# A two-layer kernel whose feed-forward transposes the next block's tokens between a block's two products

## The chip, the cores and the metric

The kernel runs on one core of a Trainium2 chip. The metric is device time in microseconds (us), the median of several runs. PE is the matmul engine (TensorE), PEld its weight loads, DVE is VectorE, ACT is ScalarE, POOL is GpSimd and SP is SyncE, which issues most of the DMA transfers.

## The reference

Two transformer-like layers on x of shape (4, 1024, 256), all in fp32, each half followed by a residual sum and a layer norm:

```python
x = _layernorm(x + ssd_forward(x, ...))          # state-space mixing, 2 heads of 128, state 64
h = gelu(x @ w1 + b1)                            # 256 -> 1024, exact gelu
x = _layernorm(x + (h @ w2 + b2))                # 1024 -> 256
x = _layernorm(x + linear_attention(x, ...))     # 16 heads, exponential features, causal in chunks
x = _layernorm(x + mixture_of_experts(x, ...))   # 2 shared experts and the best 2 of 8, 512 hidden
```

The change is in the second line pair: the feed-forward of the first layer.

## The kernel before, in words

The 4096 tokens are eight blocks of 512 tokens (`xs[i]`, token tiles of 128 on the partitions). Each block goes through five groups of steps. `ssd_block` (lines 286 to 438) is the state-space part. `ffn_block` (lines 441 to 487) is the feed-forward. `attn_front` and `attn_back` (lines 499 to 759) are the attention, in half-blocks `hb` of 256 tokens, and `attn_tail` (line 761) routes the tokens. After them come the shared experts (`shared_jobs`, line 943) and, in a stage of its own, 69 tiles of routed tokens (`slot_tiles`, line 1023), which begins 1046 us into the profiled execution.

In everything up to that stage, PE's order is written out by a planner. A `Task` (line 249) has a cost, a rank, the tasks that it comes after, each with a wait in us, and the number of PSUM banks that it takes from one of two pools: pool 0 has six banks (SSD and attention), pool 1 has two (the feed-forward, later the shared experts). `trace_tasks` (line 255) keeps a clock of its own. It always takes the task that can start first by that clock, with ties decided by the lower rank, and a bank that a task used counts as free `hold` us after the task's end. The costs and waits are numbers in the source. PE executes the resulting order strictly; the orders of DVE, ACT and POOL follow from it. A task may hand back work for a later time (`rest`): the exponentials of the attention's features, `powers` on line 591, are issued 2.5 or 1.5 us of the planner's clock behind their task.

A feed-forward block is nine tasks:

- `turn_x` (line 444): eight PE transposes bring the block's 512 tokens into `ps_txT`, two banks of pool 1 with four transposes each. ACT copies each bank into the tile `xT`, of which there is one.
- four times `hidden` (line 449): two of the eight first products each (`ps_h`, lines 453 and 456). ACT applies gelu and writes a slice of `hT`, of which there is also one.
- four times `outputs` (line 458): the eight second products of one token tile (`ps_f`, line 465). Two token tiles share a bank, and DVE adds the bank to x (line 473). The last one runs the layer norm.

`before` is the previous block in the order 0, 2, 1, 3, 4, 5, 6, 7. A block's `turn_x` comes after the last `outputs` of the block before it, and its rank is 10 + i, behind all of the attention's ranks (5 to 7). The rank of a `hidden` is 10 + i + 0.1 n, that of an `outputs` 10.5 + i + 0.1 j.

Names used later: `ps_p` (line 577) are the attention's feature products, four banks at a time, first for the keys and then for the queries, cleared by ACT (line 589) and DVE (line 587). ACT then takes exponentials of them (lines 594 and 596). `ps_sc` (line 631) are the scores, masked by DVE, in one case of four by an ACT copy and POOL (lines 640 and 641). `ps_o` (line 670) uses them. `ps_to`, `ps_oT` and `ps_w` (lines 715, 728, 735) normalise, transpose and project the result.

Of the kernel before, what the change touches and what calls it, by code (L numbers as in the profile page):

```python
# [76 lines left out]
def two_layers(ctx: ExitStack, tc: tile.TileContext, x, xT, vecs, cols, wx, w1, w2, wqkv, wout, om, rw, moe, out):  # L77
# [19 lines left out]
    def bank(name, n):  # L97

        return psum[n].tile([P, 512], F32, tag="bank", name=name)
# [100 lines left out]
    def transposed(t, i, tiles, n, engines):  # L200


        width = len(tiles) * P
        engines = list(engines)
        for c0 in range(0, KC, 512 // width):
            chunks = range(c0, min(KC, c0 + 512 // width))
            ps = bank(f"ps_t{t.name}_{c0}", n)
            at = 0
            for c in chunks:
                for j in tiles:  # L210
                    nc.tensor.transpose(ps[:, at : at + P], xs[i][:, j, c * P : (c + 1) * P], ident)
                    at += P
            engines.pop(0)(t[:, c0 : chunks[-1] + 1, :].rearrange("p c t -> p (c t)"), ps[:, :at])
        return t

    def layernorm(i, by_act=False):

        st = sm.tile([P, NT, 6], F32, tag="ln_st", name=f"ln_st{i}")
        mv = sm.tile([P, NT, 2], F32, tag="ln_mv", name=f"ln_mv{i}")
        v = sm.tile([P, NT], F32, tag="ln_v", name=f"ln_v{i}")  # L220
        for j in range(NT):
            nc.vector.bn_stats(st[:, j, :], xs[i][:, j, :])
            nc.vector.bn_aggr(mv[:, j, :], st[:, j, :])
        nc.vector.tensor_scalar_add(v, mv[:, :, 1], LN_EPS)
        r = rsqrt(v, [P, NT], "ln")
        if by_act:
            nc.vector.scalar_tensor_tensor(v, mv[:, :, 0], -1.0, r, ALU.mult, ALU.mult)
            for j in range(NT):
                nc.scalar.activation(
                    xs[i][:, j, :], xs[i][:, j, :], AF.Identity, bias=v[:, j : j + 1], scale=r[:, j : j + 1]  # L230
                )
            return
        for j in range(NT):
            nc.vector.tensor_scalar(
                xs[i][:, j, :], xs[i][:, j, :], mv[:, j, 0:1], r[:, j : j + 1], ALU.subtract, ALU.mult
            )
# [44 lines left out]


    states = [None] * NB
    ssd_end, ffn_end, proj_end, turn_end, tail_end = {}, {}, {}, {}, {}

    def ssd_block(i, wk):

# [153 lines left out]
    def ffn_block(i, before, wk):  # L441
        v = SimpleNamespace(ps=None)

        def turn_x():
            v.xT = wk.tile([P, KC, TB], F32, tag="xT", name=f"xT{i}")
            transposed(v.xT, i, range(NT), 1, (nc.scalar.copy, nc.scalar.copy))
            v.hT = wk.tile([P, HID0 // P, TB], F32, tag="hT", name=f"hT{i}")

        def hidden(ms):
            for m in ms:  # L450
                ps = bank(f"ps_h{i}_{m}", 1)
                for k in range(KC):
                    nc.tensor.matmul(  # L453
                        ps, w1_sb[:, k, m * P : (m + 1) * P], v.xT[:, k, :], start=(k == 0), stop=(k == KC - 1)
                    )
                nc.scalar.activation(v.hT[:, m, :], ps, AF.Gelu, bias=col[:, m : m + 1])  # L456

        def outputs(j):
            if j == 0:
                b2 = vec0[:, _VEC["b2"]].unsqueeze(1).to_broadcast([P, NT, D])  # L460
                nc.gpsimd.tensor_add(xs[i], xs[i], b2)
            if j % 2 == 0:
                v.ps = bank(f"ps_f{i}_{j}", 1).rearrange("p (s d) -> p s d", s=2)
            for m in range(HID0 // P):
                nc.tensor.matmul(  # L465
                    v.ps[:, j % 2, :],
                    v.hT[:, m, j * P : (j + 1) * P],
                    w2_sb[:, m, :],
                    start=(m == 0),
                    stop=(m == HID0 // P - 1),  # L470
                )
            if j % 2 == 1:
                nc.vector.tensor_add(xs[i][:, j - 1 : j + 1, :], v.ps, xs[i][:, j - 1 : j + 1, :])
            if j == NT - 1:
                layernorm(i)

        r = 10.0 + i
        last = Task(turn_x, 0.9, r, [(ssd_end[i], 10.0), (before, 0.0)], 1, 2)
        wait = 4.0
        for n in range(4):  # L480
            last = Task(lambda n=n: hidden(range(2 * n, 2 * n + 2)), 3.5, r + 0.1 * n, [(last, wait)], 1, 2, 2.2)
            wait = 0.0
        wait = 3.0
        for j in range(NT):
            last = Task(lambda j=j: outputs(j), 3.5, r + 0.5 + 0.1 * j, [(last, wait)], 1, (j + 1) % 2, 2.2)
            wait = 0.0
        ffn_end[i] = last
# [683 lines left out]
    with tc.manual_schedule(engines={mybir.EngineType.PE}):  # L1171
# [8 lines left out]
        before = None  # L1180
        ffn_order = [0, 2, 1, 3, 4, 5, 6, 7]
        for i in ffn_order:
            ffn_block(i, before, wkf)
            before = ffn_end[i]
        constants = Task(attn_constants, 0.0, 4.0, [(ssd_end[0], 0.0)])
        spaces = SimpleNamespace()

# [32 lines left out]
        last = Task(open_second, 0.0, 0.0, [(ffn_end[ffn_order[-1]], 0.0)])  # L1220
        wait, jobs = 20.0, []
        for i, _, cost, n, banks, _ in shared_jobs(early + amid, None, None, None, banks_of, 2):
            after = [(last, wait), (turn_end[i], 3.0)]
# [3 lines left out]
            last, wait = jobs[-1], 0.0  # L1227
# [31 lines left out]
        wait = 6.0  # L1259
        for _ in range(2 * NTOK // P // 8 + 1):  # L1260
            sending = Task(lambda: spaces.steps.pop(0)(), 0.0, 0.0, [(sending, wait)])
            wait = 3.6
# [14 lines left out]
    with tc.manual_schedule(  # L1277
# [7 lines left out]
        parts, n = [], -1  # L1285
# [94 lines left out]
```

## Time and profile before

| | |
|---|---|
| median of 3 runs | 1547.89 us (1545.16 to 1551.54) |
| the profiled execution, its own time | 1545.36 us |
| its span, first to last instruction | 1543.5 us |
| mean granted PE clock | 0.991 |
| PE busy | 1485.6 us, 96% of the span |
| DVE, ACT, POOL busy | 752.8, 601.4, 418.5 us |
| first routed tile (`ps_ge`) starts | 1045.9 us |
| `xT` copies on ACT | 16, median 586 ns |
| gelu's table loads on ACT (line 456) | 28, 1283 ns each |

The profiled execution is one run; its time is 1.9 us more than its span, and 2.5 us less than the median of the three timed runs. A row of the window table gives the busy time of each engine in a stretch of the span, and the granted clock of PE there. In the timeline a row stands for a merged group of instructions, and the brackets give the idle time ahead of it and what ended it. A busy PE can still be slow: at half the granted clock an instruction simply takes twice as long.

### The profile page before, as it was taken

The page shows a single profiled execution, that of the slowest core. Times are in us where ns is not written, and L with a number is a line of the kernel's source. Part 1 is how long each engine was busy: PE and PEld are TensorE (multiplying, and loading weights), DVE is VectorE, ACT ScalarE, POOL GpSimd, SP SyncE. Part 2 cuts the span into 40 slices and gives each one's busy share as a digit, 9 for nine tenths or more (in the row PEclk, how much of TensorE's full clock was granted, in tenths as well). Part 3 has the DMA queues.
Part 4 walks back from the last instruction along what each step waited for, and adds up shares of the span by engine and source line. Part 5 has one row for each costly group of instructions (what it writes and reads, how often), then busy time and mean ns, then how long its engine had stood idle before and what let it go on. Part 6 is the DMA issues. An engine that isn't in the chain of part 4 may idle for free. (4 is left out here: it accounts for less than half of the span.)

```text
span 1543.5 us, 25320 instructions
## 1 busy us (share of the span) xinstructions
PE 1485.6 (96%) x9704; PEld 964.3 (62%) x9704; DVE 752.8 (49%) x2322; ACT 601.4 (39%) x1054; POOL 418.5 (27%) x456
## 2 busy tenths in 40 slices
PE   9999989999999989999999999999999999999997
PEld 5666657666766665755766665655666666666554
DVE  6977735774757474765636364112222222222264
ACT  3465374536464546355447311112222222222132
POOL 5723302322222121222110022103444444443200
PEclk9999999999999999999999999999999999999999
DMA  9000000000000000200101061222323233232331
GB/s 330 4 1 1 1 1 1 28 2 1 29 1 22 8 20 10 97 29 1 49 8 56 15 270 44 102 76 42 48 46 46 45 48 45 46 46 37 93 102 55
DMA packets 50197, 73.54 MB, mean 48 GB/s; under 512 B 8448, under 2 KB 42752, under 8 KB 48544
## 3 DMA queue, kind: packets, MB, share of 16 engines
q1 hardware_dynamic: 36128, 52.06, 9.5%
q0 software_dynamic: 13248, 18.17, 7.7%
q8 instruction: 80, 1.31, 0.4%
q10 hardware_dynamic: 704, 1.70, 0.3%
q14 instruction: 37, 0.30, 0.1%
HBM read 45.93 MB, written 25.99 MB: 47 GB/s over the span
## 5 line engine op out<-in xcount | busy, mean ns | idle before, releaser
L1033 PE MATMUL ps_ge<-w,xeT 128*128 x552 | 248.5, 593 | 1.0 <-issue 1.0
L961 PE MATMUL ps_g<-xTs,w 128*128 128x512 f32 x512 | 228.2, 599 | 2.2 <-ACTq L1087 0.8
L961 PEld LDWEIGHTS ps_g<-xTs,w 128*128 128x128 f32 x512 | 96.8, 193 | 117.2 <-issue 107.9
L1033 PEld LDWEIGHTS ps_ge<-w,xeT 128*128 128x128 f32 x552 | 99.5, 190 | 100.6 <-issue 100.6
L1064 POOL DMA_INDIRECT acc<-ye,back x69 | 109.3, 1585 | 110.5 <-DVE xew L1020 75.9
L1043 DVE TENSOR_TENSOR ge<-se,ps_ge 128x512 f32<-128x512 f32 x69 | 47.5, 688 | 178.8 <-PE ps_ge L1033 175.9
L1055 PE MATMUL ps_ye<-w2e,geT 128*128 x552 | 130.7, 380 | 0.9 <-DVE geT L1050 0.9
L1008 POOL DMA_INDIRECT xe<-xt,sent x69 | 68.0, 986 | 228.7 <-PE ps_xe L1016 166.3
L453 PE MATMUL ps_h<-xT,w_sb 128*128 128x512 f32 x256 | 117.9, 604 | 4.8 <-ACT hT L456 4.7
L979 PE MATMUL ps_e<-w,gT 128*128 128x256 f32 x512 | 114.6, 380 | 2.1 <-DVE x L988 2.1
L465 PE MATMUL ps_f<-w_sb,hT 128*128 128x256 f32 x512 | 115.9, 380 | 0.0
L641 POOL TENSOR_TENSOR sc<-sc,mask_le 128x512 f32<-128x512 f32 x32 | 40.7, 1272 | 270.3 <-ACT sc L640 270.3
L979 PEld LDWEIGHTS ps_e<-w,gT 128*128 128x128 f32 x512 | 96.1, 190 | 18.9 <-DVE x L988 3.7
L1055 PEld LDWEIGHTS ps_ye<-w2e,geT 128*128 128x128 f32 x552 | 99.6, 190 | 12.2 <-ACT ye L1063 1.1
L465 PEld LDWEIGHTS ps_f<-w_sb,hT 128*128 128x128 f32 x512 | 95.6, 190 | 15.4 <-issue 3.4
L970 DVE TENSOR_TENSOR gT<-sl,ps_g 128x512 f32<-128x512 f32 x64 | 43.9, 686 | 122.4 <-PE ps_g L961 95.2
L969 ACT ACTIVATE sl<-ps_g 128x512 f32<-128x512 f32 x64 | 38.1, 597 | 158.2 <-PE ps_g L961 144.9
L1041 ACT ACTIVATE se<-ps_ge 128x512 f32<-128x512 f32 x69 | 41.2, 597 | 121.6 <-PE ps_ge L1033 121.6
L453 PEld LDWEIGHTS ps_h<-xT,w_sb 128*128 128x128 f32 x256 | 47.7, 193 | 57.4 <-issue 47.0
L643 DVE TENSOR_TENSOR sc<-ps_sc,mask_le 128x512 f32<-128x512 f32 x96 | 63.1, 684 | 37.3 <-PE ps_sc L631 31.6
L631 PE MATMUL ps_sc<-qf,kf 64*128 64x128 f32 x1024 | 68.3, 284 | 0.9 <-DVE kf L587 0.5
L1063 ACT ACTIVATE ye<-ps_ye,xew 128x256 f32<-128x256 f32 x69 | 32.6, 473 | 92.9 <-PE ps_ye L1055 92.9
(268 smaller groups left out, 2445.0 us busy)
## 6 DMA issues: line engine op xcount, KB each, us to landing
w<-in_moe SPq DMA_DIRECT2D x8, 1024.0 KB, 8.6
x<-in_x SPq DMA_DIRECT2D x8, 512.0 KB, 10.8
xt<-x SPq DMA_DIRECT2D x8, 512.0 KB, 3.6
td<-xTr SPq DMA_DIRECT2D x16, 256.0 KB, 2.5
w2e<-in_moe SPq DMA_DIRECT2D x8, 512.0 KB, 7.6
x<-acc SPq DMA_DIRECT2D x8, 512.0 KB, 8.8
xt<-in_xT SPq DMA_DIRECT2D x7, 512.0 KB, 11.1
out<-x SPq DMA_DIRECT2D x7, 512.0 KB, 2.9
```

Source lines behind the costliest of these rows:

```text
L453: nc.tensor.matmul(ps, w1_sb[:, k, m * P : (m + 1) * P], v.xT[:, k, :], start=(k == 0), stop=(k == KC - 1))
L465: nc.tensor.matmul(v.ps[:, j % 2, :], v.hT[:, m, j * P : (j + 1) * P], w2_sb[:, m, :], start=(m == 0), stop=(m == HID0 // P - 1),)
L631: nc.tensor.matmul(ps[s][:, r * P : (r + 1) * P], kf[rows, r, q, tok], qf[rows, r, q, tok], start=True, stop=True)
L643: nc.vector.tensor_mul(t_s, ps_s, mask)
L961: nc.tensor.matmul(ps[s], w[e][:, 2 * s + k, m * P : (m + 1) * P], xT[i][:, k, :], start=(k == 0), stop=(k == KC - 1),)
L970: nc.vector.tensor_mul(gT[i, e][:, m, :], sl, ps[1])
L979: nc.tensor.matmul(ps, gT[i, e][:, m, j * P : (j + 1) * P], w2e[:, m, :], start=(e == 0 and m == 0), stop=(e == NSH - 1 and m == HID // P ...
L1008: nc.gpsimd.indirect_dma_start(out=xe, out_offset=None, in_=xt, in_offset=bass.IndirectOffsetOnAxis(ap=sent[:, s : s + 1], axis=0),)
L1033: nc.tensor.matmul(pg[a], xeT[s][:, k, :], w13[:, bass.ds(e * (4 * HID) + (2 * a + k) * HID, HID)], start=(k == 0), stop=(k == KC - 1),)
L1043: nc.vector.tensor_mul(ge[s], se, pg[1])
L1055: nc.tensor.matmul(ps[:, :D], geT[s][:, m, :], w2[:, bass.ds(of[s] * (2 * HID) + m * D, D)], start=(m == 0), stop=(m == HID // P - 1),)
L1064: nc.gpsimd.indirect_dma_start(out=acc, out_offset=bass.IndirectOffsetOnAxis(ap=back[:, s : s + 1], axis=0), in_=ye, in_offset=None, compu ...
```

## The change

A block's `turn_x` no longer comes after the last second product of the block before, but after that block's last first product, and its rank falls by 0.8, so that at equal time it goes ahead of that block's second products. The first `hidden` of a block now waits explicitly for the last `outputs` of the block before. Nothing is computed differently, and the exponentials that are issued late are as they were.

```diff
-        last = Task(turn_x, 0.9, r, [(ssd_end[i], 10.0), (before, 0.0)], 1, 2)
+        last = Task(turn_x, 0.9, r - 0.8, [(ssd_end[i], 10.0), (hid_end.get(before), 0.0)], 1, 2)
         wait = 4.0
         for n in range(4):
-            last = Task(lambda n=n: hidden(range(2 * n, 2 * n + 2)), 3.5, r + 0.1 * n, [(last, wait)], 1, 2, 2.2)
+            after = [(last, wait)] + [(ffn_end.get(before), 0.0)] * (n == 0)
+            last = Task(lambda n=n: hidden(range(2 * n, 2 * n + 2)), 3.5, r + 0.1 * n, after, 1, 2, 2.2)
             wait = 0.0
+        hid_end[i] = last
...
-            before = ffn_end[i]
+            before = i
```

Since the planner's clock decides what comes next, the order of everything behind the second block's `turn_x`, attention and shared experts included, is drawn up anew.

More of the change, by code (lines that the diff above doesn't have):

```diff
@@ L283, in two_layers @@
     states = [None] * NB
-    ssd_end, ffn_end, proj_end, turn_end, tail_end = {}, {}, {}, {}, {}
+    ssd_end, hid_end, ffn_end, proj_end, turn_end, tail_end = {}, {}, {}, {}, {}, {}
     def ssd_block(i, wk):
```

## The prediction

> **What bounds the kernel now.** I read the page first:
>
> ```profile
> span 1543.5 us, 25320 instructions
> PE 1485.6 (96%) x9704; PEld 964.3 (62%) x9704; DVE 752.8 (49%) x2322; ACT 601.4 (39%) x1054; POOL 418.5 (27%) x456
> ...
> PE   9999989999999989999999999999999999999997
> ```
>
> PE is busy for 96% of the span, and in no stretch below 70%. The change moves PE instructions and removes none, so it can only touch the 58 us in which PE is idle, and what its clock loses. Next the window table, over the stretches in which the PE timeline shows its longer gaps:
>
> ```profile
> core 0: us, PE busy (x) PEld busy (x) DVE busy (x) ACT busy (x) POOL busy (x), PEclk, DMA share, GB/s
> 184.00:220.00 36.00, 29.66 (x214) 16.51 (x215) 16.26 (x36) 31.08 (x43) 3.26 (x2) 0.91 0.00 1
> 325.00:355.00 30.00, 25.41 (x164) 15.43 (x164) 18.58 (x41) 17.43 (x28) 8.32 (x8) 0.94 0.00 1
> 430.00:450.00 20.00, 18.19 (x195) 10.72 (x196) 8.10 (x15) 17.83 (x27) 5.91 (x6) 1.00 0.01 1
> 595.00:615.00 20.00, 17.42 (x105) 10.98 (x105) 10.08 (x24) 17.20 (x25) 4.56 (x4) 1.00 0.02 1
> 680.00:697.00 17.00, 14.49 (x75) 8.15 (x74) 9.27 (x28) 15.36 (x23) 1.27 (x1) 0.92 0.01 0
> 805.00:825.00 20.00, 17.10 (x90) 9.20 (x83) 12.03 (x31) 19.13 (x28) 0.00 (x0) 0.91 0.15 52
> ```
>
> Where PE idles, ACT is mostly 86 to 96% busy, against 39% over the span. These are the places where feature exponentials, gelus (or the shared experts' activations) and the table loads between them fall together. The granted clock is 0.91 to 0.94 in four of them. Third, one such place in the timelines of PE and ACT:
>
> ```profile
> 193.01 1.09 PE L562 MATMUL ps_qkT<-ident,qk 128*128 128x128 f32 x8
> 196.04 5.32 PE L453 MATMUL ps_h<-xT,w_sb 128*128 128x512 f32 x8 [1.94 <-ACT hT L456]
> ```
>
> ```profile
> 193.28 0.71 ACT L596 ACTIVATE kf<-kf,ecap 128x512 f32<-128x512 f32 x1
> 194.00 1.28 ACT L456 ACT_TABLE_LOAD   x1
> 195.30 1.26 ACT L456 ACTIVATE hT<-ps_h,col 128x512 f32<-128x512 f32 x2
> ```
>
> ```profile
> 196.00:200.00 4.00, 3.96 (x6) 1.78 (x7) 0.54 (x1) 3.97 (x6) 0.00 (x0) 0.58 0.01 4
> ```
>
> PE stands for 1.94 us until a gelu frees a bank; the gelu stands behind exponentials and a table load. Then PE runs at 0.58 of its clock for 4 us, which loses another 0.42 x 4 = 1.7 us. Such a dip takes 1.7 us off 50 us, so a 50 us window with one has clock 0.97; five such windows have 0.97 and one (650 to 700) has 0.93: seven dips, 12 us. Last, PE's waits by releaser:
>
> ```profile
> PE ps_h L453 <- ACT hT L456: 4.7, 3, 2.0
> PE ps_o L670 <- POOL sc L641: 4.1, 2, 2.6
> PE ps_p L577 <- DVE kf L587: 3.2, 2, 2.5
> PE ps_oT L728 <- DVE o L721: 3.1, 2, 2.7
> PE ps_txT L211 <- DVE x L473: 2.0, 2, 1.7
> ```
>
> What this change aims at is the last row: a turn that waits for the second products' bank, 2.0 us in all. The planner keeps 4.0 us between turn and first product, but at block 2 the trace has the last transposes ending at 136.9 us and the first products from 137.2 us: nothing is lost there.
>
> **The change part by part.** Nothing is added to PE: per turn the same 8 transposes and 2 ACT copies of 586 ns, no DMA, nothing on POOL. In the instruction order of the changed kernel the seven later turns stand 23 to 43 us of PE work ahead of their block's first products, where it was 0.5 to 6 us. The last second product of block 7 comes some 20 us of PE work earlier, and with it SP's loads of the shared experts' weights; their first products have other work in front of them in either order. In the last part the order is looser: the dispatch's products (line 932) stand 14 us of PE work later, with 40 us left to the first routed tile. In the trace they ended at 993 us and the 512 KB loads of `w2e` that they release were issued by 997 us and landed in 12.3 us at most. So 40 us cover this; without cover it would be up to 16 us. ACT gets 90 table loads for 88, 2.6 us, beside PE.
>
> The rest is counted by cover: the PE work, in start-to-start times of the trace of before (0.86 us for a 512-wide fp32 product, 3.45 for eight second products, 0.49 for four transposes), that stands between producer and consumer, in both orders. The waits that should go:
>
> - The turn's wait for the bank of the second products: 0.35 us (block 1) and 1.67 us (block 6). 2.0 us.
> - At 213.9 us PE waits 2.56 us for POOL's masked scores; cover 4.0 us becomes 7.6. With the dip behind it 2.6 + 1.7 = 4.3 us.
> - At 252.5 us `ps_oT` waits 2.70 us with 1.2 us of cover, made up of block 3's turn; the new order has 3.7 there. 2.7 us.
> - At 335.7 us the query features wait 2.51 us for banks of the key features: cover 1.95 becomes 4.4. With the dip 4.2 us.
> - At 560.6 us and 645.3 us `ps_w` waits 1.76 and 1.20 us behind covers of 0 and 2.6; both become 5.05. 3.0 us.
>
> Together 16.2 us. The waits that should come:
>
> - A block's second products now stand behind the turn, in a bank that the turn's first copy must clear. For turns 3, 6 and 7 there are 3 to 6 us of cover; for turns 2, 1, 4 and 5 only the second four transposes, 0.49 us. With ACT free the copy takes 0.59 us and a start of some 0.1, so at least 0.2 to 0.3 us is lost. But ACT is in order: ahead of the copy at turn 4 stand two gelus and four copies (wait 0.8 us), at turn 5 a clearing of features, a table load of 1.28, an exponential of 0.72 and another clearing, 3.8 us against 1.0 of PE work (wait 2.7 us). I take 0.3 + 0.4 + 0.8 + 2.7 = 4.2 us; bounds 1.2 (ACT free) and 8 (two waits more like turn 5's). Behind PE's waiting instruction all of attention's products stand.
> - Does a wait of 2.7 us bring a dip? The trace says yes: of the waits of 1.9 us and more listed here all but the one at 252.5 us were followed by one. The Trainium skill, "TensorE: Matmul & The Clock Gate", section "What's actually happening", says that half rate comes after at least one idle window of about 3.4 us; by that rule neither this wait nor any listed here would cost more than itself. With the rule the sum below would be 12.8 us gone against 10.5 come, a gain of 2.3 us instead of 0.6; the measured dip decides. 1.7 us.
> - In half-block 9, `ps_oT` follows `ps_to` with 0.22 us of cover. In the trace 1.94 us passed without a wait and 1.2 waited 2.7; so 1.7 to 3.7 us, taken at 2.0 since DVE is less loaded there, plus a dip, 3.7 us.
> - Scores to `ps_o`: covers 1.9, 2.6 and 2.6 at three tiles, where 2.9 passed in the trace: 1.7 us.
> - Block 1's hidden products still fall among the features of half-blocks 0 and 1, now with 3.3 us between products in one bank instead of 4.3: 1.0 us more.
> - Hot ACT stretches: six before and six after, elsewhere. Counted by the measured durations of what ACT has to do between two of PE's instructions, the worst goes from 27.6 to 29.2 us of ACT work in 25 us of PE work: 1.6 us and a dip, 3.3 us.
>
> Together 4.2 + 1.7 + 3.7 + 1.7 + 1.0 + 3.3 = 15.6 us. Of the table loads a page speaks too: "ScalarE: Activation LUTs", section "What ACT_TABLE_LOAD costs", has 1283 ns and a drain of 1380 for each. The trace agrees on the load, but the exponential before it ended at 193.99 and the gelu began at 195.30: no drain is to be seen. By the page turn 5 would wait 4.1 us instead of 2.7; I keep the trace.
>
> Sum: 1545.4 (the profiled execution) - 16.2 + 15.6 = 1544.8 us. That execution was 2.5 us under the median of the runs, so 1547.3, say 1547 us.
>
> **The rivals.** *Faster: the new places do not stall.* Only the copies at the turns cost (5.9 us), and the other 9.7 us stay covered, because the real PE runs slower than the planner's clock and so gives more cover than asked. Then -16.2 + 5.9 = -10.3, 1537.6 us. For it speaks that covers of 1.94 us passed three times at `ps_oT`; against it the count of hot ACT stretches, six and six.
>
> *Slower: the stalls belong to ACT, not to the order.* ACT's stretches of features, gelus and table loads are as many as before, so each of the four attention waits that I let go (14.2 us) returns at another consumer in the same stretch, and only the turn's 2.0 us are gained. Then -2.0 + 15.6 = +13.6, 1561.5 us. It decides from 58% of the 14.2 us on: (7.7 + 0.6) / 14.2. For it speaks the window table, in which the gaps follow ACT's load whatever the consumer; against it the waits at 252.5 and 560.6 us, which were plain lack of cover.
>
> *The change does not do what it says*: the turn was no wait worth speaking of, the first products still wait for the second ones of the block before, and the reshuffle cancels. That is part of the middle case.
>
> **How the numbers follow.** About 0.5%, 7.7 us, is what a measurement of this kernel can tell from no change. The middle case (-0.6 us, its own range 1540 to 1555) has 0.41, the slower one 0.34, since an order that is drawn up anew also holds waits that I did not find, while I listed those of before in full; the faster one 0.25. The range of 1534 to 1560 reaches most of the way to both ends: all the new waits hidden but the copies' lower bound (-16.2 + 1.2, 1532.9) and all attention waits returned (1561.5).
>
> **What would show it.** In the profile of the changed kernel: the row of `ps_txT` waiting for DVE's x is gone; `ps_f` has waits for ACT's xT copy, 4 us in total, the longest at block 4's first second product; `ps_oT` has one wait of about 2 us some 630 us in; PE busy less dips is as before, with five to nine dips. The first `ps_ge` starts between 1038 and 1053 us and the rest takes 498 us as now. It would be wrong if `ps_ge` starts before 1038 (the faster case), or if `ps_h`, `ps_p` and `ps_k` wait longer in total than before while ACT's stretches stay above 90% (the slower case).

## The result, and the profile after

The changed kernel takes 1574.18 us (median of 5 runs, 1573.29 to 1577.03), against 1545.16 us for the kernel before on the same chip: 1.0184 times as long, 95% interval 1.0168 to 1.0200. The forecast was 1547 us, with a range of 1534 to 1560. It was wrong: the change costs some 28 us. The page of the changed kernel has

```profile
span 1571.4 us, 25316 instructions
PE 1498.6 (95%) x9704; PEld 971.2 (62%) x9704; DVE 750.5 (48%) x2322; ACT 606.0 (39%) x1056; POOL 419.1 (27%) x456
...
PE   9999989998899998989989999999999999999998
...
PEclk9999989999999999999999999999999999999999
```

The span is 27.9 us longer. PE has the same 9704 matmuls, but stands idle for 72.8 us instead of 57.9 (+14.9) and is busy for 1498.6 us instead of 1485.6 (+13.0). Equal work that takes longer is a matter of the clock: a first product's matmul takes 429 ns from start to start, and 853 in a stretch at half rate. In the trace's clock records before the routed tiles, the kernel before has 7 such stretches, each of 3.4 us, 24 us in all; the changed one has 12, six of them of 6.8 us, 61 us in all. PE is busy for 54 us of them instead of 23. Half of the difference, 15 us, is an estimate of what they cost, enough for the 13.0.

The first `ps_ge` starts at 1073.9 us instead of 1045.9. What follows takes 497.5 us, as it did. All of the loss thus lies in the part whose order the planner writes. PE's waits there, by what released them (total us, times, longest us):

```profile
PE ps_f L465 <- ACT xT L213: 8.1, 4, 5.7
PE ps_k L656 <- DVE qkT L567: 6.3, 4, 2.3
PE ps_g L964 <- ACT sl L972: 3.9, 3, 1.8
PE ps_oT L731 <- DVE o L724: 3.8, 4, 2.3
PE ps_w L738 <- ACT oT L733: 3.8, 2, 2.1
PE ps_e L982 <- DVE gT L973: 3.3, 1, 3.3
PE ps_k L656 <- DVE kf L590: 3.3, 1, 3.3
```

The row of `ps_txT` waiting for x is gone, as intended. In its place stands the second product's wait for the turn's copy, 8.1 us. Four more rows have grown or are new. In the kernel before, three of them were

```profile
PE ps_k L653 <- DVE qkT L564: 2.7, 1, 2.7
PE ps_w L735 <- ACT oT L730: 1.8, 1, 1.8
PE ps_g L961 <- ACT sl L969: 0.2, 1, 0.2
```

and `ps_e` had only its 2.1 us for x. Of waits over 1.5 us there are 15 with 36.3 us, where there were 13 with 27.1 (the one of 1.5 us at the kernel's very start, in both, is left out here and below).

The window table, over stretches of 50 us and of 20:

```profile
core 0: us, PE busy (x) PEld busy (x) DVE busy (x) ACT busy (x) POOL busy (x), PEclk, DMA share, GB/s
350.00:400.00 50.00, 43.81 (x417) 32.72 (x417) 28.33 (x71) 23.11 (x37) 9.67 (x9) 0.93 0.01 1
650.00:700.00 50.00, 42.55 (x418) 26.66 (x418) 25.43 (x65) 30.95 (x47) 6.50 (x7) 0.90 0.07 23
495.00:515.00 20.00, 16.26 (x123) 9.83 (x121) 10.36 (x24) 19.87 (x29) 1.77 (x2) 0.91 0.08 27
578.00:598.00 20.00, 14.05 (x73) 7.98 (x72) 14.87 (x39) 18.72 (x27) 3.34 (x3) 0.89 0.07 27
667.00:687.00 20.00, 14.99 (x72) 8.36 (x71) 12.99 (x36) 18.88 (x26) 3.52 (x3) 0.83 0.07 26
```

Before, the worst window of 50 us had a clock of 0.93; now three have 0.90 and three 0.93, of which the first two rows are examples. ACT is 46 and 62% busy in these two, but 94 to 99% in the three rows of 20 us, as it was in such places before. This parts the long waits in two. Those that end within some 20 us in which ACT is over 90% busy were 8 with 17.8 us before, and are 8 with 17.1 us now, at other places of the order. All other waits over 1.5 us rose from 9.3 to 19.1 us, and two of them, 5.7 and 3.3 us long, are 9.0 us, nearly the whole of that rise. These two come next.

**Turn 5, the longest wait.** The timelines of PE, ACT and DVE:

```profile
349.99 1.15 PE L580 MATMUL ps_p<-qkT,om_sb 32*128 32x256 f32 x16
351.07 1.09 PE L211 MATMUL ps_txT<-ident,x 128*128 128x128 f32 x8
357.85 5.42 PE L465 MATMUL ps_f<-w_sb,hT 128*128 128x256 f32 x16 [5.69 <-ACT xT L213]
```

```profile
351.20 0.69 ACT L592 ACTIVATE kf<-ps_p,fcap 128x512 f32<-128x512 f32 x1 [4.67 <-PE ps_p L580]
351.90 1.28 ACT L597 ACT_TABLE_LOAD   x1
356.02 0.72 ACT L597 ACTIVATE kf<-kf,fbias 128x512 f32<-128x512 f32 x1 [2.84 <-DVE kf L590]
356.65 0.67 ACT L592 ACTIVATE kf<-ps_p,fcap 128x512 f32<-128x512 f32 x1
357.22 1.06 ACT L213 COPY xT<-ps_txT 128x512 f32<-128x512 f32 x2
```

```profile
352.52 1.77 DVE L527 TENSOR_SCALAR ss<-ss 128x64 f32<-128x64 f32 x1
355.19 0.80 DVE L590 TENSOR_SCALAR kf<-ps_p,fcap,ffloor 128x512 f32<-128x512 f32 x1
```

Read it from the end. PE's second product waits for the copy; ACT had the transposes from 352 us on, but in front of the copy stands an exponential, which waits 2.84 us for the features that DVE clears; and DVE clears them only at 355.19, behind the norm of the queries and keys. Three queues, each in order, hand on the delay: PE stands behind ACT and ACT behind DVE, and neither PE's nor ACT's own work makes it. Then PE runs slowly:

```profile
355.00:362.00 7.00, 4.15 (x11) 3.42 (x12) 4.33 (x11) 4.10 (x7) 2.07 (x2) 0.55 0.01 2
```

**The shared experts, at the end.** One wait lies in a part that the forecast had called covered:

```profile
968.72 3.19 PE L982 MATMUL ps_e<-w,gT 128*128 128x256 f32 x14
975.23 4.98 PE L982 MATMUL ps_e<-w,gT 128*128 128x256 f32 x14 [3.33 <-DVE gT L973]
```

```profile
970.63 1.21 DVE L908 TENSOR_TENSOR in_lane<-lane_no,lane 128x1024 f16<-128x1024 f32 x1
971.77 1.67 DVE L900 TENSOR_TENSOR in_tile<-tile_no,its 128x568 f16<-128x568 f32 x1
973.37 1.21 DVE L908 TENSOR_TENSOR in_lane<-lane_no,lane 128x1024 f16<-128x1024 f32 x1
974.50 0.67 DVE L973 TENSOR_TENSOR gT<-sl,ps_g 128x512 f32<-128x512 f32 x1
```

PE's gate products end at 968.9, and the last product `gT` that DVE makes of them starts 5.6 us later, behind the comparisons that build the dispatch's masks. The rows of those comparisons, before and after (duration min/median/max in ns, first and last start in us):

```profile
L905 DVE TENSOR_TENSOR in_lane<-lane_no,lane x8: 1205/1212/1549, 916.4 to 935.5; 128x1024 f16<-128x1024 f32 x8
```

```profile
L908 DVE TENSOR_TENSOR in_lane<-lane_no,lane x8: 1204/1212/1772, 954.0 to 973.4; 128x1024 f16<-128x1024 f32 x8
```

Before, they were done at 937 us, while the gate products of a block still had 9 us to go:

```profile
937.35 8.85 PE L961 MATMUL ps_g<-xTs,w 128*128 128x512 f32 x20 [0.45 <-DVE gT L970]
```

Now they reach 5.7 us past the end of such a block. From 950 to 972 us DVE has no free moment:

```profile
950.00:972.00 22.00, 21.91 (x58) 10.67 (x57) 22.00 (x35) 3.58 (x6) 13.13 (x7) 1.00 0.68 275
```

### The profile page after: what moved, and what is told of

It reads as the page before. It is cut to its first block, busy times and chain, and to the rows that moved or that the text cites. A ratio compares the mean times of both kernels' runs of the same rounds, so it can differ in the third digit from the quotient of the medians.

```text
span 1571.4 us, 25316 instructions
## 1 busy us (share of the span) xinstructions
PE 1498.6 (95%) x9704; PEld 971.2 (62%) x9704; DVE 750.5 (48%) x2322; ACT 606.0 (39%) x1056; POOL 419.1 (27%) x456
## 5 line engine op out<-in xcount | busy, mean ns | idle before, releaser
L465 PE MATMUL ps_f<-w_sb,hT 128*128 128x256 f32 x512 | 119.7, 389 | 8.1 <-ACT xT L213 8.1
L634 PEld LDWEIGHTS ps_sc<-qf,kf 64*128 64x128 f32 x1024 | 61.9, 194 | 11.2 <-issue 5.6
## 6 DMA issues: line engine op xcount, KB each, us to landing
xt<-in_xT SPq DMA_DIRECT2D x7, 512.0 KB, 11.1
```

The costliest lines, as they stand in the source:

```text
L465: nc.tensor.matmul(v.ps[:, j % 2, :], v.hT[:, m, j * P : (j + 1) * P], w2_sb[:, m, :], start=(m == 0), stop=(m == HID0 // P - 1),)
L634: nc.tensor.matmul(ps[s][:, r * P : (r + 1) * P], kf[rows, r, q, tok], qf[rows, r, q, tok], start=True, stop=True)
```

## The experiments

All times are medians; the ratio is to the kernel before, measured beside it, with its 95% interval. "Over before" in the text is the ratio less one, times 1545.2 us, so that kernels measured at different times can be set side by side; two such values are told apart from some 4 us on.

| kernel | us | ratio |
|---|---|---|
| after | 1574.18 | 1.0184 (1.0168, 1.0200) |
| e2 new order, turns at their old place | 1576.97 | 1.0192 (1.0164, 1.0220) |
| e5 old order, turns moved | 1557.23 | 1.0075 (1.0058, 1.0092) |
| e9 as e5, turns in pool 0 | 1552.11 | 1.0046 (1.0030, 1.0063) |
| e18 after, turns in pool 0 | 1564.01 | 1.0110 (1.0085, 1.0134) |
| e3 after, copies on VectorE | 1577.47 | 1.0204 (1.0177, 1.0231) |
| e4 / e6 after / before, exponentials at once | 1565.58 / 1556.66 | 1.0128 (1.0100, 1.0155) / 1.0076 (1.0059, 1.0092) |
| e15 / e16 after / before, exponentials 0.5 us late | 1568.44 / 1551.19 | 1.0136 (1.0113, 1.0159) / 1.0040 (1.0019, 1.0061) |
| e10 / e11 after / before, Relu | 1546.88 / 1534.66 | 1.0001 (0.9990, 1.0012) / 0.9928 (0.9910, 0.9946) |
| e13 / e14 as e5 / as e2, Relu | 1533.62 / 1549.92 | 0.9912 (0.9891, 0.9934) / 1.0018 (1.0009, 1.0027) |
| e7, e8 before, one planner number changed | 1550.97, 1553.41 | 1.0036 (1.0022, 1.0050), 1.0043 (1.0026, 1.0060) |
| e12 after, floor on GpSimd | 1576.04 | 1.0195 (1.0174, 1.0215) |
| e17 after, no lane masks | 1571.74 | 1.0166 (1.0141, 1.0191) |

### e1, e5 and e2: the move and the order, each alone

The change does two things: it puts seven turns elsewhere, and it makes the planner draw up everything behind them anew. To part them, a hand-written step moves or puts back the turns after the planner is done. The loop itself is the same in e1 and e5:

```diff
+        for x, y in zip(ORDER, ORDER[1:]):
+            order.remove(turns[y])
+            at, cover = order.index(firsts[x]) + 1, 0.0
+            while cover < 2.2 and order[at] is not seconds[x]:
+                cover += order[at].cost
+                at += 1
+            order.insert(at, turns[y])
+            turns[y].start, turns[y].end = order[at - 1].start, order[at - 1].end   # e5 only
```

> PE's order of before, in which only the seven later turns are taken out and put behind the last first product of the block before (two tasks or so behind it, at the latest ahead of that block's second products). Theory A, the redrawn order of all the rest costs the time: 1541 to 1553 us, since the turn alone brings its copies' waits (about 4 us) and saves 2. Theory B, the turn between the two products costs it, through the bank that its copy must clear: 1565 to 1577 us, with ps_f waiting 8 us or more for ACT's xT.

e1 came to 1569.48 us, 1.0145. But in e1 a moved turn kept its planned start, and the late exponentials go by that clock, so that some were issued at wrong points and the kernel no longer computes the same. It decides nothing here. e5 gives the moved turn the start of its new neighbour.

> As the first kernel of the turn moved alone, but with the moved turn given the planned time of its new place, so that the late exponentials keep their places. Theory A (the redrawn order costs the time, the turn's place does not): 1543 to 1556 us, with ps_f waiting 4 to 8 us for ACT's copies. Theory B (the turn between the products is a cost of its own besides the order): 1560 to 1572 us.

e5: 1557.23 us, 11.6 us over before, between the two theories' ranges. The second products wait for ACT's copy in it as well:

```profile
PE ps_f L488 <- ACT xT L214: 10.0, 4, 4.5
```

e2 takes the new order and puts the turns back behind the last second product of the block before.

```diff
+        for x, y in zip(ORDER, ORDER[1:]):
+            order.remove(turns[y])
+            order.insert(order.index(ffn_end[x]) + 1, turns[y])
```

> PE's order of after, in which only the seven later turns are put back behind the last second product of the block before. Theory A (redrawn order): 1560 to 1572 us; only ps_f's 8 us and the half-rate stretch behind the longest of them go, and some waits at the first products come. Theory B (the turn): 1541 to 1552 us.

e2: 1576.97 us, 29.7 over before, no less than the changed kernel itself (28.4), and more than either theory gave it. Two of its waits:

```profile
PE ps_txT L212 <- DVE x L491: 6.3, 7, 3.4
PE ps_kv L732 <- DVE state L726: 5.3, 4, 1.7
```

In the new order the two places of the turn are worth the same: the old one waits 6.3 us for DVE's x, and its cover is missing at `ps_kv`; the new one waits 8.1 us for ACT's copy. So the move as such loses little there, but gains nothing either, and the order around it carries the loss.

### e3, e9 and e18: the copy and its bank

```diff
-            transposed(v.xT, i, range(NT), 1, (nc.scalar.copy, nc.scalar.copy))
+            transposed(v.xT, i, range(NT), 1, (nc.vector.tensor_copy, nc.vector.tensor_copy))      # e3
+            transposed(v.xT, i, range(NT), 0 if i else 1, (nc.scalar.copy, nc.scalar.copy))         # e9 and e18
```

> After, with the turn's two copies on VectorE instead of ScalarE; PE's order is that of after. Theory B (the second products stand behind ScalarE's queue): ps_f waits under 3 us for the copies instead of 8.1, and 1555 to 1565 us. Theory A (redrawn order): the same fall of ps_f's waits, but 1566 to 1576 us, since those waits and what follows them are a third of the loss at most.

e3: 1577.47 us. Both theories had the wait shrink; it keeps its place and its size:

```profile
PE ps_f L465 <- DVE xT L213: 8.9, 4, 5.5
```

This agrees with the timelines of turn 5: DVE, with its norm in front, is what ACT waits for there, so the copy is as late on either. Nor do the exponentials' delays make it: e4 below has PE's order of after and no delays, and the wait is 7.5 us. No run here moves the norm itself.

> The turn moved alone, as e5, with the seven moved turns' transposes in banks of the six of pool 0 instead of the feed-forward's own two; PE's order is the same. Theory B1, what the turn costs by itself is that second products need the bank which its copy must clear: ps_f's waits for the copies (10.0 us in e5) vanish and the time is 1545 to 1551 us. Theory B2, the copies cost because they take ScalarE's and PE's time at a bad place: 1554 to 1560 us as e5.

e9 (e5 with the turns in the attention's six banks): 1552.11 us, 7.1 over before where e5 had 11.6. The 10.0 us of `ps_f` are gone, and part of them returns as turns that wait for an attention bank: `ps_txT` 3.2 us for ACT's lT and 2.7 for its xTa. It lies between the two theories' ranges.

> The changed kernel with the turns of all blocks but the first in the attention's pool of six banks instead of the second products' pool of two; PE's order is the same. Theory: the wait of 5.69 us at turn 5 and the half clock of 6.8 us behind it belong to the shared bank, and with the three smaller waits (8.1 us in all) they go: 6 to 11 us less than after, so 1563 to 1568. Rival: ACT is late there whatever the bank, and the wait returns at the next product that needs ACT or an attention bank, as half of it did in the old order with the turns moved alone: 1569 to 1574.

e18: 1564.01 us, 17.0 over before, 11.4 less than the changed kernel (the spans of the two profiled executions are 8.7 apart), within the theory's range. `ps_f` waits for nothing any more; of its waits

```profile
PE ps_txT L211 <- ACT sc L643: 3.9, 1, 3.9
PE ps_k L656 <- DVE state L703: 3.6, 1, 3.6
```

are new. The shared bank is thus the largest part of the loss that one edit takes out without leaving anything out of the kernel: some 11 us, with an uncertainty of some 4. Its size comes from the place in the queues, not from the bank alone: 8.1 us of waits and the slow clock behind them.

### e4, e6, e15 and e16: exponentials late or not

```diff
-            return (2.5, 1.5)[s], powers
+            powers()                          # e4 on after, e6 on before
+            return (0.5, 0.5)[s], powers      # e15 on after, e16 on before
```

> After, with the features' exponentials issued in the same step as the clearing of their banks instead of 1.5 to 2.5 us later; PE's order is that of after. Theory C, the late exponentials come to stand ahead of gelus and copies in the new order: the time falls to 1555 to 1566 us. Theory A: no gain, 1570 to 1585 us, because exponentials issued at once stand ahead of other clearings just as well.

> Before, with the features' exponentials issued at once; PE's order is that of before. Theory C, the late exponentials were tuned to the old order and hurt in the new one: slower than before here, 1552 to 1565 us, where the same edit made the changed kernel 8.6 us faster. Theory A, the late exponentials matter little beside the order: 1541 to 1550 us.

> The changed kernel with its exponentials issued 0.5 us of the planner's clock behind their task, in place of 2.5 and 1.5; PE's order is the same. By ACT's instruction order, 11 of the 32 feature sets are then cut by a gelu or silu, where it was 20, and none with the exponentials at once (1565.6 us, 8.6 under after). Theory: the time goes with the cuts, less what lateness saves; 1561 to 1568 us. Rival: lateness by itself is what costs, cuts or not; then half way between, 1568 to 1573, or as after, 1574.

> The kernel before with its exponentials issued 0.5 us behind their task. Cut feature sets 6 where it was 13; at once (none cut) it took 1556.7 us, 11 more than before. If cuts cost as much here as in the changed kernel, fewer of them with some lateness left give 1535 to 1545 us and a version that beats both; if the lateness of 1.5 to 2.5 us is what saves, 1550 to 1556.

Over before, in us, by the lateness of the exponentials:

| | at once | 0.5 us | 2.5 and 1.5 us |
|---|---|---|---|
| old order | 11.7 | 6.2 | 0 |
| new order | 19.8 | 21.0 | 28.4 |
| difference | 8.1 | 14.8 | 28.4 |

In the old order issuing them late saves 11.7 us; in the new one the same delays cost 8.6. So some 20 of the 28 us, give or take 5, hang on delays that suit the old order. e4 and e6 lie in theory C's ranges, e15 on the border of its two and e16 in its second. How a delay goes wrong, the timelines of after show some 590 us in:

```profile
589.29 1.28 ACT L456 ACT_TABLE_LOAD   x1
590.58 1.26 ACT L456 ACTIVATE hT<-ps_h,col 128x512 f32<-128x512 f32 x2
591.86 1.28 ACT L599 ACT_TABLE_LOAD   x1
593.16 0.72 ACT L599 ACTIVATE qf<-qf,ecap 128x512 f32<-128x512 f32 x1
```

```profile
593.91 0.49 DVE L600 TENSOR_SCALAR qf<-qf,elow 128x512 f32<-128x512 f32 x1 [2.71 <-ACT qf L599]
594.32 1.52 DVE L590 TENSOR_SCALAR kf<-ps_p,fcap,ffloor 128x512 f32<-128x512 f32 x2
```

```profile
595.18 1.12 PE L656 MATMUL ps_k<-ident,kf 128*128 128x128 f32 x4 [3.25 <-DVE kf L590]
```

A pair of gelus with two table loads cuts through the four late exponentials of one set of features. DVE's floor of the second exponential waits 2.71 us for them, DVE's clearing of the next half-block's features stands behind the floor, and PE waits for that. By ACT's instruction order, 13 of the 32 sets are cut in the kernel before, 20 in the changed one. The count alone is no measure, however: in the old order the kernel with 13 cut sets is the fastest of three, ahead of those with 6 and none. What stands in front of whom must count for more than how often. That cuts as such are the mechanism is therefore not shown.

### e10, e11, e13 and e14: without table loads

```diff
-                nc.scalar.activation(v.hT[:, m, :], ps, AF.Gelu, bias=col[:, m : m + 1])
+                nc.scalar.activation(v.hT[:, m, :], ps, AF.Relu, bias=col[:, m : m + 1])
...
-            nc.scalar.activation(sl, ps[0], AF.Silu)
+            nc.scalar.activation(sl, ps[0], AF.Relu)
```

6 table loads remain of 88 or 90. One activation takes the same time with either function, 687 ns behind the first products and 597 in the shared experts, so that the loads are all that ACT saves.

> After, with relu in place of the feed-forward's gelu and of the shared experts' silu, which leaves those two functions out; relu needs no table load, so that ScalarE's loads fall from 90 to 6, and nothing else changes in PE's order. Theory F, the loss is gelus and silus with their table loads that cut into the late exponentials: within 8 us of the same kernel made from before. Theory G, the loss is missing cover in PE's order whatever ScalarE does: 18 us or more above it.

> Before, with the same relu in place of gelu and silu, loads from 88 to 6. Both theories: faster than before, 1515 to 1538 us, as the stretches where ScalarE is over 90% busy lose up to a quarter of their work. It is the comparison for the last kernel.

> The kernel of e5 (the order of before, seven turns moved alone) with Relu in place of Gelu and Silu, which leaves those functions out, and with them all but 6 table loads. To be read beside 1534.7 us (before with Relu) and 1546.9 (after with Relu), which are 12.2 apart. Theory: what is left of the loss without tables is the moved turn itself, its bank of the second products that ACT's copy must clear; the move alone cost 11.4 us with the tables, so 1543 to 1547 us here. Rival: the turn stalls only because ACT is full of table loads; then 1535 to 1539, and the 12 us belong to the new order.

> The kernel of e2 (the new order with its turns put back behind the last second product) with Relu in place of Gelu and Silu, which leaves those functions out. Theory: the new order costs time only through the gelus and silus that cut into the late exponentials; without tables it is as good as the old one but for the 6 us that its turns wait for VectorE's bank, so 1535 to 1541 us, against 30 us over before with the tables. Rival: the new order has waits of its own, whatever the tables; then 1545 us or more, as after with Relu.

Over before: e11 (old order) -11.1, e13 (old order, turns moved) -13.6, e14 (new order, turns back) +2.8, e10 (after) +0.2. e10 is thus 11.3 above e11, between theory F's 8 and theory G's 18. Measured from e11, the moved turns alone are worth -2.5 us, which cannot be told from nothing, where they cost 11.6 with the loads; the new order alone costs 13.9 where it cost 29.7; both cost 11.3 where it was 28.4. My theory for e13 and e14, that the 12 us left without loads belong to the turn, fell: they belong to the order. And in the old order the moved turns cost time only while ACT has table loads to do: their waits fall from 10.0 to 4.3 us. In the new order turn 5 stalls as before, though there is no load in front of its copy:

```profile
PE ps_f L465 <- ACT xT L213: 6.5, 4, 5.7
```

So at turn 5 it is DVE's norm, as the timelines said, and not the load between.

### e7 and e8: how much an order is worth

```diff
-        wait = 4.0
+        wait = 3.5      # e7: turn to first product
...
-            last = Task(lambda n=n: hidden(range(2 * n, 2 * n + 2)), 3.5, r + 0.1 * n, [(last, wait)], 1, 2, 2.2)
+            last = Task(lambda n=n: hidden(range(2 * n, 2 * n + 2)), 3.6, r + 0.1 * n, [(last, wait)], 1, 2, 2.2)      # e8
```

> Before, with the planner's wait between a turn and its first products at 3.5 us instead of 4.0. The turn stays where it was in principle, but the order is redrawn in a seventh of its places. Theory D, the old order is a lucky or picked one and any redrawing costs: 1555 to 1580 us. Theory E, it is this change's order that is bad: 1540 to 1552 us.

> Before, with the planner's cost of a pair of first products at 3.6 us instead of 3.5 (the trace has 3.44 to 3.7). A smaller redrawing. Theory D: 1550 to 1570 us. Theory E: 1540 to 1552 us.

5.6 and 6.6 us over before. Each lets the planner draw another order, and that is all that it does. e7 lies in theory E's range and e8 just above it, so that neither theory is ruled out; but neither redraw costs a quarter of what this change's does. e7 even has the same wait of the shared experts, 3.3 us of `ps_e` for DVE's gT.

### e12 and e17: DVE's queue

```diff
-                        nc.vector.tensor_scalar_max(f[r], f[r], elow[:, s : s + 1])
+                        nc.gpsimd.tensor_scalar_max(f[r], f[r], elow[:, s : s + 1])      # e12
```

> After, with the floor under the features (the maximum behind every second exponential) on GpSimd instead of VectorE; PE's order is that of after. Theory F1, the late exponential holds up VectorE's queue, in which the clearing of the next feature banks stands behind that maximum (the wait of 3.25 us of ps_k): 1558 to 1567 us. Theory F2, ScalarE's queue alone is what matters: 1570 to 1580 us, since GpSimd takes longer for the same maximum.

e12: 1576.04 us, in theory F2's range. The wait of `ps_k` for DVE's kf, 3.3 us, is gone, but `ps_o` now waits 7.6 us for POOL's masked scores, where it was 2.5. The floor takes 1.56 us on POOL and took 0.49 on DVE. Taking that one link out of DVE's queue only moved the delay to POOL's.

```diff
+        nc.gpsimd.memset(in_lane, 0.0)
...
-            wide = [P, group, P]
-            nc.vector.tensor_tensor(
-                in_lane[:, g, :],
-                lane_no.unsqueeze(1).to_broadcast(wide),
-                lane[:, n, ts].unsqueeze(2).to_broadcast(wide),
-                ALU.is_equal,
-            )
```

> The changed kernel without the eight VectorE comparisons of 1.2 us that build the dispatch's lane masks (the masks are zero, so the dispatch's lists of tokens are left out with them; the work of the routed tiles stays the same in size). In the trace of after VectorE is busy without a break from 950 to 972 us with these and the tile masks, a product of the shared experts comes 5.5 us after PE's, and PE waits 3.33 us at 971.9 and then loses about 1.6 us of clock; in every kernel with the new order the wait is there with 3.32 or 3.33 us, in none with the old order. Theory: the new order puts the masks in front of the shared experts' products; without eight of the sixteen the wait goes and the first routed tile starts at 1068.5 to 1069.5 us instead of 1073.9. Rival: the wait is for something else on the way (the shared weights, the activation), or another takes its place; then the first routed tile starts at 1072 to 1074.

e17's timeline of PE at the shared experts has no wait left, nor a dip there:

```profile
948.62 21.21 PE L958 MATMUL ps_g<-xTs,w 128*128 128x512 f32 x48
969.67 13.98 PE L976 MATMUL ps_e<-w,gT 128*128 128x256 f32 x64
```

The first `ps_ge` starts at 1070.8 us, 3.1 earlier than in the changed kernel, short of the 4.4 to 5.4 expected: two waits have come that after did not have, 1.06 us at 946.5 and 1.00 at 1046.1. The median is 2.4 us lower, less than the 4 us that can be told apart. So the masks make that wait, as its absence shows; it is worth about 3 us as measured, 5 with its dip if nothing came in its place.

No kernel here that computes the same beats the kernel before; e11 and e13, which leave gelu and silu out, are faster.

## Why the prediction was wrong

**The step that failed.** In the forecast's own terms PE's idle time was to fall by 2.3 us (12.8 of waits gone, 10.5 come), and the clock was to cost 1.7 us more. Measured are 14.9 us more of idle time, 9.2 of them in waits over 1.5 us, and 13.0 us of longer work. The sum priced each wait alone: those that go at the consumers that had waited before, those that come by the queue of one engine. For all else that a new order brings it had 3.3 us ("hot ACT stretches").

**Right.** The row of `ps_txT` for x went. The waits at 252.5 and 335.7 us went. The wait of `ps_oT` foretold at some 630 us with 2.0 us came at 649.4 with 2.27, and a dip behind it. The routed tiles take 497.5 us, foretold as 498, and ACT has its two table loads more.

**"I take 0.3 + 0.4 + 0.8 + 2.7 = 4.2 us; bounds 1.2 and 8."** The place was right, block 4's first second product, the size not: the four waits are 0.71, 1.40, 0.34 and 5.69 us, 8.1 together, above the upper bound. The term for turn 5 counted what ACT itself has to do in front of the copy, 3.8 us. It did not ask what ACT's exponential waits for: DVE's clearing, which stands behind the norm. e3, e4 and e10 bear this out. Taken with its clock, the term of 4.2 + 1.7 = 5.9 us measured some 11 (e18).

**"A dip, 1.7 us."** That waits of some 2 us can bring half rate was right: the first stretch of after stands behind a wait of 1.70 us at 201.4. That nearly all do was misread: in the trace of before the wait of 2.02 us that ends at 603.4, one of the `ps_h` row, brought none either, nor did one of 1.96 that ends at 350.3. "TensorE: Matmul & The Clock Gate" of the Trainium skill, section "What's actually happening", gives a free-running window of 3.413 us, and the stretches of all kernels here, ahead of the routed tiles, are about one, two or three times that; all but one of the long waits of after are shorter than such a window. What the forecast had not seen, since the trace of before had only single ones, is the double. Five to nine dips were foretold; 12 stretches came, six of them double. PE's busy time, foretold as unchanged but for dips, grew by 13.0 us, nearly half of the loss; the forecast had it at one dip more.

**"Waits that should go: 16.2 us."** Covers were compared at consumers that had waited before, as if the rest of the order stayed. But where ACT is full, the waits stayed what they were (17.8 and 17.1 us) and only changed their places. `ps_w`, booked as 3.0 us gained, waits 3.8 us in two new places, for a copy on ACT that stands behind late exponentials into which two gelus or a silu cut, with two table loads each time (399 to 403 and 798 to 801 us); of the `ps_o` gain, 2.5 us of POOL's 4.1 remain and a wait of 2.5 us for ACT's copied scores has come. These are new meetings of queues (gelu against late exponentials, floor against clearing), found only where each engine's order is followed through to the others. The 3.3 us for "hot ACT stretches" were meant to hold all of that; e4 and e6 put the part that hangs on late exponentials at 20 us.

**"The dispatch's products stand 14 us of PE work later ... 40 us cover this."** For PE's products this held. The DVE comparisons that make their masks moved along, in front of the shared experts' `gT`, and were not costed: 3.33 us and a dip. The rule was in the forecast's own method (what is queued behind it on its engine?) and was not applied to DVE.

**The rivals.** The slower one, waits that return at other consumers in ACT's full stretches (1561.5 us), was the nearest. Its sign came: `ps_h`, `ps_p` and `ps_k` together wait 22.7 us instead of 19.5, and there are still stretches in which ACT is busy for over 90%. It was 13 us short for what lies outside of them. At turn 5 ACT is 46% busy over 50 us and waits for DVE, and at the shared experts DVE is busy for all of 22 us and ACT for 3.6. The sentence that "an order that is drawn up anew also holds waits that I did not find" carried the truth but had no price: e7 and e8 give one, some 6 us for a redraw that does nothing else. And the range reached only to 1560.

**Open.** e18 and e17 account for some 11 and 3 of the 28 us. The other 14 or so are spread over other waits, of at most 3.3 us, and their slow clock; the runs say that they vanish in part with the table loads and in part with the exponentials' delays, but not which wait takes how much of it. The two are not independent, so their 17 and 20 us must not be added.

## What to carry to other kernels

When a change lets a scheduler redraw an order, price the redraw itself before the thing moved: change a number that means nothing and measure it. For each new wait follow the chain one engine further than the engine that PE waits for; a queue that is half idle can still be late because its head waits for a third one. And delays fitted by hand, here those of the exponentials, belong to the order they were fitted to; after a redraw they are new unknowns.

## Of the hardware

Half rate came in stretches of 3.4 us and, in the changed kernel, six times of 6.8. Eleven of its twelve stand at a wait of 1.7 to 5.7 us; the one at 501.3 us has four short waits ahead of it, 1.8 us together. e4, e6, e12, e13, e16 and e18 have one stretch of 10.2 each. So a wait of 2 us can cost 1.7 us more, or twice that, or nothing: four waits of 1.6 to 1.9 us in the changed kernel and three of 2.0 to 2.7 in the kernel before brought none. What decides, no run here shows. DVE's comparison of 128x568 elements to f16 took 0.73 us at 967.24, while POOL stood still, and 1.67 us at 971.77, while POOL multiplied a tile of the same kind; if the one comes from the other, which no run here tries, part of the backlog in front of the shared experts is due to it. And Relu in place of gelu and silu, with 82 table loads fewer, was worth only 11 us to the kernel before, though the loads take 82 x 1.28 = 105 us of ACT: nearly all of them were hidden.
